# Layer 0 two groups ahead of the pairs, doubled tiles, and xe one group early in the second stage: a four-layer graph network on one core

## The chip, the cores and the metric

One core of one Trainium2 chip. The metric is the device time of one execution in microseconds (us). Times are medians of repeated executions.

## The reference, cut to what matters

Input: x, 128 graphs of 128 nodes with 128 features, and adj, an integer matrix of relations for each graph. Each of the four layers is x = x + layer(max(layernorm(x), 0), adj). Only the first two matter here:

```python
# layer 0: for each relation r = 1..7
mask = (adj == r); degree = max(mask.sum(axis=2), 1e-6)
agg += ((mask / degree) @ h) @ rel_weights[r]
out = relu(layernorm(agg + h @ self_w.T + self_b) * gamma + beta)

# layer 1: for all pairs (i, j) of nodes
D = abs(h[:, :, None, :] - h[:, None, :, :])
s = W2 . leaky(batchnorm(D @ W1.T + b1)) + b2      # batchnorm over ALL graphs and pairs
A = softmax(where(adj > 0, s, -9e15)); y = A @ h ...
```

The batch norm needs the statistics of all pairs before the first score. The kernel therefore makes the pairs twice: in the **first stage** for statistics (woven with layer 0), in the **second stage** for scores. Layers 2 and 3 are the **third stage**.

## The kernel before

Work goes in 32 groups of four graphs (k = 0 to 3). A scheduler orders the instructions of each engine when the kernel is built, and gives out buffers; it follows the order of the program only roughly. The parts that the change touches:

```python
def pre_norm(pool, src, mv=None, rs=None):
    ...
    h = pool.tile([P, G, P], F32, tag="hn", bufs=1, name="hn")
    norm(h, src, mv, rs)
    nc.vector.tensor_scalar(h, h, 0.0, None, op0=OP.max)
    return h

def around(pool, hT):                        # h with its first 64 nodes appended again
    xe = pool.tile([P, G, P + 2 * KH], F32, name="xe")
    nc.gpsimd.tensor_copy(xe[:, :, 0:P], hT)
    nc.gpsimd.tensor_copy(xe[:, :, P:], hT[:, :, 0:2 * KH])
    return xe

def pairwise(pool, xe, k, t):                # one pair step: 16 of them in a group
    d = pool.tile([P, 2, KC, P], F32, tag="d", bufs=3, name="d")
    ...
    eng = nc.gpsimd if t in ON_POOL else nc.vector      # ON_POOL = {1}: one d in four
    eng.tensor_tensor(d, ahead, x[...].to_broadcast(...), OP.subtract)
    nc.scalar.activation(d, d, AF.Abs)
    ...                                      # matmuls of d with w1T into hp (two buffers)

# layer0(g), cut: p0 has two buffers, unless a tile says bufs=1
for k in range(G):
    mask = p0.tile([P, 7, P], F32, name="mask", bufs=1)
    nc.vector.tensor_tensor(mask, adjT[...], rel[...], OP.is_equal)
    for r0, r1 in ((0, 3), (3, 7)):
        yield
        ...                                  # ph = h x relw (TensorE), hw = copy of ph (ScalarE)
        yield
        for r in range(r0, r1):
            nc.tensor.matmul(pa[:, r - r0, :], mask[:, r, :], hw[:, r - r0, :], ...)
        if r0 == 0:
            for r in range(7):               # the degrees
                nc.tensor.matmul(pa[:, 3, r:r + 1], mask[:, r, :], ones[:, 0:1], ...)
            ...                              # rdeg = 1 / max(degree, 1e-6) (VectorE)
        yield
        ...                                  # o += pa * rdeg (VectorE)

def pairs(g):
    xe = around(p0, HT[g])
    for k in range(G):
        yield from pair_stats(p0, xe, k, g * G + k)

for _ in layer0(0):
    pass
for g in range(NG):                          # 4 steps of layer 0 after each pair step
    _weave(pairs(g), layer0(g + 1) if g + 1 < NG else iter(()), 4)
```

## Time and profile before

| | before |
|---|---|
| median, us | 6777.6 |
| first stage: one group, steady (us between two xe copies) | 98.9 |
| VectorE busy in it / idle, us | 76.1 / 23.0 |
| second stage: one group, us | 64.94 |
| granted TensorE clock, steady first stage / second stage | 0.78 / 0.98 |

The views behind the table are in the prediction. In a timeline line, the columns are start and length in us, engine, line of the program, operation, tile written and tiles read, shapes, count, and in brackets the idle time of the engine before it and what ended it. Names of tiles come without the number of the buffer or the group. d holds the differences of pairs, hp their products with w1T and st the statistics of hp; pa holds the products with mask; hn is a normed tile, and lnrs and RS are the factors for a norm, which GpSimd makes.

### The profile page before, as it was taken

To read this page: it belongs to the slowest core of one execution; us is meant where nothing else is said; L and a number is where in the kernel's file an instruction comes from. 1 tells how busy PE (TensorE), PEld (TensorE's weight loads), DVE (VectorE), ACT (ScalarE), POOL (GpSimd) and SP (SyncE) were. 2 spreads that over 40 slices of the span, in tenths; PEclk is the share of its full clock that TensorE was granted. 3 is DMA by queue.
4 is the path that set the end of the run, shared out by engine and by line. 5 is a ranking of instruction groups with operands and counts; after the bars stand their busy time and mean duration, and the time that the engine had idled before them with its cause. 6 is when DMAs were issued, how large, how long until landed. Compare 5 with 4: busy or idle time off the path is not lost.

```text
span 6785.6 us, 58156 instructions
## 1 busy us (share of the span) xinstructions
PE 5091.2 (75%) x21510; PEld 2364.6 (35%) x21510; DVE 4731.7 (70%) x8187; ACT 3135.1 (46%) x2690; POOL 1536.1 (23%) x754
## 2 busy tenths in 40 slices
PE   5766776676677667666899999999999666666666
PEld 3323332332333233232222222222222355555555
DVE  5777777777777777778666666666666566666666
ACT  2333333333333333333677777777777422222222
POOL 2222222222222222222222222222222100000000
PEclk7887877787787778777899999999999877766667
DMA  0000000000000000000000000000000000000000
GB/s 21 5 10 10 8 7 10 10 5 10 10 8 7 10 10 5 10 7 5 15 16 16 16 16 19 16 16 17 17 18 16 16 13 13 13 13 13 13 13 8
DMA packets 108922, 81.32 MB, mean 12 GB/s; under 512 B 23392, under 2 KB 92256, under 8 KB 108640
## 3 DMA queue, kind: packets, MB, share of 16 engines
q1 hardware_dynamic: 91744, 69.20, 3.5%
q10 hardware_dynamic: 16896, 8.39, 0.4%
q8 instruction: 173, 2.83, 0.2%
q14 instruction: 109, 0.89, 0.0%
HBM read 47.36 MB, written 30.21 MB: 11 GB/s over the span
## 4 chain that ended last, share of the span: by engine, by line
PE 45%; DVE 30%; POOL 11%; ACT 9%; issue 4%; DMA 0%; SPq 0%; POOLq 0%; DVEq 0%; ACTq 0%
PE hp L193 20%; DVE d L187 9%; POOL d L187 6%; ACT d L189 5%; PE ps L376 5%; PE pa L264 3%; PE pv L526 3%; PE pa L261 3%; PE pt L165 3%; PE ph L255 2%; ACT z L372 2%; DVE st L203 2%; POOL xe L175 2%; DVE st L205 2%; PE pk L383 2%
## 5 line engine op out<-in xcount | busy, mean ns | idle before, releaser
L193 PE MATMUL hp<-d,w1T 128*64 128x512 f32 x8192 | 2553.4, 684 | 673.0 <-ACT d L189 541.7
L189 ACT ACTIVATE d<-d 128x2048 f32<-128x2048 f32 x1024 | 1938.8, 1906 | 935.6 <-POOL d L187 451.2
L187 DVE TENSOR_TENSOR d<-xe 128x2048 f32<-128x2048 f32 x768 | 1964.2, 2561 | 479.7 <-PE hp L193 477.1
L187 POOL TENSOR_TENSOR d<-xe 128x2048 f32<-128x2048 f32 x256 | 1096.6, 4284 | 3036.2 <-PE hp L193 3007.7
L193 PEld LDWEIGHTS hp<-d,w1T 128*64 128x64 f32 x8192 | 649.6, 152 | 2280.9 <-issue 1447.5
L372 ACT ACTIVATE z<-hp,bias,scale 128x1024 f32<-128x1024 f32 x512 | 608.4, 1200 | 352.9 <-PE hp L193 352.7
L376 PE MATMUL ps<-z,w2z 128*32 128x512 f32 x2048 | 508.4, 608 | 93.3 <-ACT z L372 93.3
L257 ACT COPY hw<-ph 128x384 f32<-128x384 f32 (+1 forms) x256 | 135.6, 530 | 857.0 <-PE ph L255 857.0
L203 DVE BATCH_NORM_STATS2 st<-hp 128x6 f32<-128x512 f32 x512 | 352.7, 689 | 229.6 <-PE hp L193 229.6
L261 PE MATMUL pa<-hw,mask 128*128 128x128 f32 x1792 | 325.7, 328 | 244.4 <-DVE mask L249 216.5
L261 PEld LDWEIGHTS pa<-hw,mask 128*128 128x128 f32 x1792 | 262.7, 221 | 514.4 <-issue 376.8
L135 POOL TENSOR_SCALAR lnrs<-lnmv 128x4 f32<-128x4 f32 x128 | 37.6, 294 | 1600.2 <-DVE lnmv L143 1600.2
L165 PE MATMUL pt<-ident,e 128*128 128x128 f32 x768 | 150.5, 344 | 292.4 <-ACT e L510 232.8
L165 PE MATMUL pt<-ident,hn 128*128 128x128 f32 x512 | 125.7, 392 | 298.7 <-DVE hn L159 234.5
L205 DVE BATCH_NORM_STATS2 st<-hp 128x6 f32<-128x512 f32 (+1 forms) x512 | 332.3, 649 | 0.0
L255 PE MATMUL ph<-relw,h 128*128 128x384 f32 (+1 forms) x512 | 305.1, 683 | 0.0
L270 DVE SCALAR_TENSOR_TENSOR o<-pa,rdeg,o 128x128 f32<-128x128 f32 x896 | 292.9, 336 | 12.5 <-PE pa L261 11.8
L148 DVE TENSOR_SCALAR hn<-x,lnmv,lnrs 128x128 f32<-128x128 f32 x384 | 111.8, 355 | 238.1 <-POOL lnrs L136 238.1
L264 PEld LDWEIGHTS pa<-ones,mask 128*128 128x128 f32 x1792 | 259.0, 229 | 0.0
L264 PE MATMUL pa<-ones,mask 128*128 128x1 f32 x1792 | 252.8, 270 | 0.0
L166 ACT COPY h<-pt 128x512 f32<-128x512 f32 x64 | 37.5, 586 | 432.2 <-PE pt L165 432.2
L175 POOL COPY xe<-h 128x512 f32<-128x512 f32 x64 | 154.3, 2410 | 353.9 <-DVE d L187 209.4
(154 smaller groups left out, 5222.6 us busy)
## 6 DMA issues: line engine op xcount, KB each, us to landing
x<-x SPq DMA_DIRECT2D x128, 256.0 KB, 2.4
u<-rows SPq DMA_DIRECT2D x32, 384.0 KB, 3.3
x<-in_x_dram SPq DMA_DIRECT2D x32, 256.0 KB, 2.7
adj<-in_adj_dram SPq DMA_DIRECT2D x32, 256.0 KB, 2.8
out_dram<-x ACTq DMA_DIRECT2D x32, 256.0 KB, 2.3
rows<-sk SPq DMA_DIRECT2D x32, 130.0 KB, 2.8
rows<-zero SPq DMA_DIRECT2D x2, 384.0 KB, 3.9
relw<-in_rel_w_dram SPq DMA_DIRECT2D x1, 448.0 KB, 4.0
```

Source lines behind the costliest of these rows:

```text
L165: nc.tensor.transpose(pt[:, k, :], src[:, k, :], ident)
L187: eng.tensor_tensor(d, ahead, x[:, None, None, :].to_broadcast([P, 2, KC, P]), OP.subtract)
L189: nc.scalar.activation(d, d, AF.Abs)
L193: nc.tensor.matmul(hp[64 * hh:64 * hh + 64, c:c + 512], w1T, d[:, hh, c:c + 512], start=True, stop=True)
L203: nc.vector.bn_stats(st[:, 2 * t, :], hp[:, 0:512])
L205: nc.vector.bn_stats(st[:, 2 * t + 1, :], hp[:, 512:1024 - P * last])
L255: nc.tensor.matmul(ph[:, 0:r1 - r0, :], hT[:, k, :], relw[:, r0:r1, :], start=True, stop=True)
L261: nc.tensor.matmul(pa[:, r - r0, :], mask[:, r, :], hw[:, r - r0, :], start=True, stop=True)
L264: nc.tensor.matmul(pa[:, 3, r:r + 1], mask[:, r, :], ones[:, 0:1], start=True, stop=True)
L270: nc.vector.scalar_tensor_tensor(o[:, k, :], pa[:, r - r0, :], rdeg[:, r:r + 1], o[:, k, :], op0=OP.mult, op1=OP.add)
L372: nc.scalar.activation(z, hp, AF.Prelu, bias=bias1, scale=scale1[:, 0:1], alpha=0.01)
L376: nc.tensor.matmul(ps[q:q + 32, :], w2z[:, w:w + 32], z[:, 512 * c:512 * c + 512], start=j < 4, stop=j >= 4, skip_group_check=True)
```

## The change

The intent: run layer 0 two groups ahead of the pairs, so that xe is ready long before it is needed; give the tiles of layer 0 a second buffer; and make xe of the second stage a group early.

```diff
+AHEAD = 2
...
-        h = pool.tile([P, G, P], F32, tag="hn", bufs=1, name="hn")
+        h = pool.tile([P, G, P], F32, tag="hn", name="hn")
...
-        xe = pool.tile([P, G, P + 2 * KH], F32, name="xe")
+        xe = pool.tile([P, G, P + 2 * KH], F32, name="xe", bufs=AHEAD + 1)
...
-                mask = p0.tile([P, 7, P], F32, name="mask", bufs=1)
+                mask = p0.tile([P, 7, P], F32, name="mask")
# ... the same for adj, adjf, adjT and o
...
             transpose(hT, h)
+            yield
+            XE[g] = around(p0, hT)

         def pairs(g):
-            xe = around(p0, HT[g])
+            xe = XE.pop(g)
...
-        for _ in layer0(0):
-            pass
+        XE = {}
+        for g in range(AHEAD):
+            for _ in layer0(g):
+                pass
         for g in range(NG):
-            _weave(pairs(g), layer0(g + 1) if g + 1 < NG else iter(()), 4)
+            _weave(pairs(g), layer0(g + AHEAD) if g + AHEAD < NG else iter(()), 4)
...
+        XE = {0: around(p1, HT[0])}            # second stage
         def group_scores(g):
-            xe = around(p1, HT[g])
+            if g + 1 < NG:
+                XE[g + 1] = around(p1, HT[g + 1])
+            xe = XE.pop(g)
```

Since `pre_norm` is shared, hn is doubled in the later stages too.

More of the change, by code (lines that the diff above doesn't have):

```diff
@@ L227, in layer0 @@
             nc.sync.dma_start(x, a["x"][bs].rearrange("b t c -> t b c"))
-            adj = p0.tile([P, G, P], I32, name="adj", bufs=1)
+            adj = p0.tile([P, G, P], I32, name="adj")
             nc.sync.dma_start(adj, a["adj"][bs].rearrange("b t s -> t b s"))
@@ L232, in layer0 @@
             yield
-            adjf = p0.tile([P, G, P], F32, name="adjf", bufs=1)
+            adjf = p0.tile([P, G, P], F32, name="adjf")
             nc.vector.tensor_copy(adjf, adj)
@@ L237, in layer0 @@
             yield
-            adjT = p0.tile([P, G, P], F32, name="adjT", bufs=1)
+            adjT = p0.tile([P, G, P], F32, name="adjT")
             transpose(adjT, adjf)
             yield
-            o = p0.tile([P, G, P], F32, name="o", bufs=1)
+            o = p0.tile([P, G, P], F32, name="o")
             po = sm("po")
```

## The prediction

> **What bounds the kernel now.** I began with busy time in long stretches, to see the stages. Columns: matmul, weight load, VectorE, ScalarE, GpSimd busy us (with counts), granted TensorE clock, DMA share, GB/s.
>
> ```profile
> core 0: us, PE busy (x) PEld busy (x) DVE busy (x) ACT busy (x) POOL busy (x), PEclk, DMA share, GB/s
> 140.00:3100.00 2960.00, 2071.99 (x8259) 924.07 (x8255) 2275.45 (x4159) 1069.73 (x808) 804.49 (x389) 0.79 0.03 8
> 3250.00:5430.00 2180.00, 1968.42 (x8186) 646.84 (x8183) 1401.62 (x1443) 1601.76 (x1176) 581.32 (x197) 0.98 0.06 16
> 5560.00:6785.00 1225.00, 793.47 (x4031) 647.27 (x4029) 786.02 (x2038) 340.17 (x582) 73.55 (x108) 0.69 0.04 12
> ```
>
> The first stage (layer 0 woven with the pair statistics, to about 3219 us) has no full engine: VectorE 77%, matmuls 70%. The second is matmul bound (90%, clock 0.98). The third is a chain of short steps. The change is meant for the first, so I next read the chain of work that ended last around one group boundary.
>
> ```profile
> 1739.71 1.13 PE pt L165 x4
> ...
> 1740.86 0.59 ACT h L166
> ...
> 1741.51 4.21 POOL xe L175
> 1745.72 0.34 POOL xe L176
> 1746.07 4.15 POOL d L187
> ...
> 1750.24 3.72 ACT d L189 x2
> ...
> 1754.00 6.52 PE hp L193 x16
> ```
>
> This is a start-up that each group pays: the last transpose of layer 0 for group g+1 lands on ScalarE, GpSimd copies it to xe, GpSimd makes a difference d, ScalarE takes its absolute value, and then sixteen matmuls run at 0.41 us each. The same matmuls take 0.24 us each once running (eight in 1.94 us). xe copies follow each other at 98.9 us (1741.51, then 1840.56), 31 times. One such period, and VectorE's waits in it (us in total, times, longest):
>
> ```profile
> 1741.50:1840.56 99.06, 69.39 (x276) 30.96 (x276) 76.10 (x140) 35.74 (x27) 26.94 (x14) 0.78 0.03 9
> ```
> ```profile
> DVE st L203 <- PE hp L193: 7.0, 7, 1.7
> DVE hn L148 <- POOL lnrs L136: 5.2, 1, 5.2
> DVE rdeg L266 <- PE pa L264: 5.1, 4, 2.4
> DVE mask L249 <- PE pa L261: 3.4, 2, 2.2
> DVE o L148 <- POOL lnrs L136: 1.2, 1, 1.2
> DVE hn L148 <- POOL RS L136: 0.9, 1, 0.9
> ```
>
> VectorE is busy 76.1 of 99.1 us and idle 23. About 9.7 us of that idle lies at the boundary (the 5.2, 1.2, 0.9, and 2.3 of the waits for hp); the other 13 lie in the middle, in layer 0's exchange with TensorE. Busy time itself holds waiting. In the timeline of both engines:
>
> ```profile
> 1765.15 5.07 DVE L187 TENSOR_TENSOR d<-xe 128x2048 f32<-128x2048 f32 x1
> ```
> ```profile
> 1763.54 4.54 POOL L187 TENSOR_TENSOR d<-xe 128x2048 f32<-128x2048 f32 x1 [12.02 <-PE hp L193]
> ```
>
> A VectorE d normally takes 2.2 us. This one took 5.07, because GpSimd's d ran to 1768.1 and VectorE needed 2.2 us after that. The d at 1817.98 (4.64 us) is the same; with a norm slowed beside GpSimd's mask (1.60 instead of 1.11 us), such stalls are 5.7 us a period. Net VectorE work is thus 76.1 - 5.7 = 70.4 us.
>
> **What the Trainium skill says.** "SBUF — State Buffer", section "Who interferes with whom": a VectorE instruction with two SBUF inputs and a GpSimd instruction that reads SBUF exclude each other for a whole instruction. The trace agrees (5.07 against 2.2 us; and the xe copy above took 4.21 us behind two VectorE d, 0.61 us in the second stage). "TensorE: Matmul & The Clock Gate", section "What's actually happening": idle TensorE falls to half clock and needs a few us of work to come back. The trace agrees: 0.41 us a matmul after 5.28 us of idle, 0.24 in dense stretches. "Perfetto Trace Analysis", section "Optimization Strategy": a consistent bubble can mean too few buffers. Here it is at first order not a lack of buffers but of distance, since layer 0 of g+1 ends just when pairs of g end.
>
> **The change part by part.** No instruction is added or removed in the first stage. It makes layer 0 run two groups ahead, copies xe at the end of layer 0 (three xe buffers), and doubles hn, adj, adjf, adjT, o and mask. The diff does not show the order, because a scheduler fixes it, so I compared the built instruction order of both kernels. In the changed one, a steady period on GpSimd reads: d of k=0, 1, 2, then two rsqrt and the mask of layer 0, the xe copy for two groups on, a third rsqrt, then d of k=3. VectorE's first d of a group no longer follows the xe copy of that group, two masks are made back to back before TensorE needs them, and the norm of the next layer 0 stands among the last pair steps.
>
> (1) Boundary. 9.7 us of VectorE idle a group should go nearly whole: xe is at hand a group early, and the 5.2 us wait for lnrs arose because GpSimd did xe and d first.
> (2) Middle. The waits for mask (3.4) should go with the second mask buffer; those for rdeg and hp (5.1 and 4.7) should shrink, since they are waits for TensorE at half clock or held up by masks. I leave 5 us of the 13.
> (3) Port. GpSimd still does four d of 4.17 us and now meets a denser VectorE. In the pairs-only end of the stage (3138 to 3205 us) each k has one VectorE d of 4.1 to 5.1 us, a stall of up to 2.9. By walking the new order by hand with the durations above, I find stalls at three of the four d (2.7, 1.5, 1.6), plus some at mask and norm, together 7 to 8 us instead of 5.7.
> Sum: 70.4 + 7.6 + 5 = 83 us a period. The hand walk, with all matmuls at full speed, came to 80; 83 allows for half-clock stretches.
>
> The whole stage. Before: pairs of group 0 start at about 82 us, those of group 31 end at about 3219, so 3137 us. After, from the same start: group 0 has to carry two layers 0 (groups 1 and 2), at 21 us of VectorE work and some TensorE latency more, so 83 + 28; groups 1 to 29 take 83; groups 30 and 31 have pairs alone, at 16.5 us per k, so 66 each; 5 for seams. 111 + 29 x 83 + 132 + 5 = 2655. Gain 3137 - 2655 = 482 us.
>
> (4) Second stage. The xe copy there waits 7.2 us for a buffer, but takes 0.6 us, ends 4 us before the next GpSimd d, and is not on the chain. Bringing it a group early is worth nothing. With hn doubled, VectorE's 2.0 us wait for py per group disappears, and the norm (1.4 us) moves to a place where VectorE idled 2.25 us for hp; both are beside a TensorE that is 90% busy. In the built order, TensorE and ScalarE are unchanged from the start of that stage on. I count 0, plus or minus 15 us.
> (5) Third stage. It gets the second hn too; its order is the same on all engines, and no wait for the hn buffer shows there. 0.
>
> 6777 - 482 = 6295.
>
> **The rivals.**
> A, only the boundary goes. The layer 0 exchange in the middle keeps its 13 us of idle. For it: most of the order there is unchanged, and rdeg waits for TensorE, not for a buffer. Against: mask waits are 3.4 of the 13, and matmuls run at half clock after gaps, which shrink together. Period 70.4 + 6 + 13 = 89, stage 30 x 89 + 165 = 2835, time 6475.
> B, GpSimd's queue becomes the wait. d of k=3 stands behind two rsqrt, the mask and the xe copy, which itself waits for the last transpose and then for three VectorE d in a row (6.6 us). If the pairs starve there, the bubble is only moved from the boundary into k=2. For it: the queue is in order and 98.9 us periods show how firmly such a chain locks. Against: three VectorE d are already made ahead of it, enough for about 10 us of pairs. Period 87 to 90, time about 6415 to 6505.
> C, VectorE fills up entirely. Period 76 (net work plus stalls), 30 x 76 + 165 = 2445, time 6085. An in-order queue that waits for TensorE rarely gets there; pairs alone keep 1.9 us of idle per k even without layer 0.
> D, nothing: the transfers and copies were hidden anyway. The chain passes through xe at each of 31 boundaries, so I hold this for the second stage only.
>
> **Range and chances.** Each us of the period is 30 us of the time. Periods from 79 to 88 give 6175 to 6445; I state 6180 to 6450. A gain of 2% is 136 us, which a period under 94.5 gives; even rival B is well below. Faster 0.95, same 0.04, slower 0.01.
>
> **What would show it.** Step 1: distance between xe copies near 83 us instead of 98.9; the chain no longer has xe; no 5 us wait for lnrs. Step 2: mask gone from the list of waits, clock of the stage above 0.79. Step 3: VectorE busy 77 to 79 us a period, with d of 4 to 5 us. Steps 4 and 5: the second stage stays at about 64.9 us a group, the third at its length. I am wrong if VectorE waits at k=2 or 3 for hp while GpSimd's xe copy stands over 5 us, if the granted clock stays below 0.8, or if the second stage moves by more than 30 us.

## The result

6699.9 us (6693.6 to 6712.5) against 6777.6 us. Ratios here are the mean time of one kernel's fast runs over that of the other's of the same rounds, so not quite the ratio of the medians; here it is 0.9888 (95% interval 0.9871 to 0.9906). That is 1.1% faster: outside the predicted range, and by the 2% measure the same.

From the traces, by stage (us):

| | before | after | difference |
|---|---|---|---|
| last pair statistic of the first stage starts at | 3215.6 | 3127.2 | -88.4 |
| from there to the first z of the second stage | 24.9 | 26.4 | +1.5 |
| first z to last z | 2087.1 | 2099.4 | +12.3 |
| last z to first yT of the third stage | 28.3 | 28.1 | -0.2 |
| from there to the end | 1429.7 | 1429.6 | -0.1 |

A steady group of the first stage takes 95.57 us instead of 98.9. First its busy times (columns as in the prediction), then VectorE's waits in it:

```profile
1155.70:1251.27 95.57, 63.40 (x276) 28.10 (x276) 78.58 (x140) 35.58 (x27) 30.75 (x14) 0.86 0.03 9
```
```profile
DVE st L204 <- PE hp L194: 7.1, 6, 2.4
DVE rdeg L267 <- PE pa L265: 5.0, 3, 2.4
DVE hn L149 <- POOL lnrs L137: 1.5, 1, 1.5
DVE o L149 <- POOL lnrs L137: 1.2, 1, 1.2
DVE mask L250 <- PE pa L262: 1.1, 1, 1.1
```

VectorE is idle for 17.0 us (95.57 - 78.58), where 5 were predicted. Against before, the 5.2 us wait for lnrs became 1.5 and the mask waits went from 3.4 to 1.1; the waits for hp and rdeg did not move. VectorE's busy time rose from 76.1 to 78.6 us with the same 140 instructions, so some of them now take longer. The timelines of GpSimd and VectorE show what became of the lnrs wait:

```profile
1155.70 6.87 POOL L176 COPY xe<-h 128x512 f32<-128x512 f32 x1 [3.48 <-ACT h L167]
...
1163.57 1.04 POOL L137 TENSOR_TENSOR lnrs<-lnrs,mhalf 128x4 f32<-128x4 f32 x1
1164.58 4.16 POOL L188 TENSOR_TENSOR d<-xe 128x2048 f32<-128x2048 f32 x1
```
```profile
1155.42 6.68 DVE L188 TENSOR_TENSOR d<-xe 128x2048 f32<-128x2048 f32 x3
...
1164.64 4.69 DVE L149 TENSOR_SCALAR hn<-x,lnmv,lnrs 128x128 f32<-128x128 f32 x3 [1.48 <-POOL lnrs L137]
...
1181.76 3.19 DVE L160 TENSOR_SCALAR hn<-hn 128x512 f32<-128x512 f32 x1
...
1232.37 3.41 DVE L188 TENSOR_TENSOR d<-xe 128x2048 f32<-128x2048 f32 x1
```

The xe copy, 0.6 us of work, stands behind three VectorE d. Then GpSimd's d starts 0.06 us before VectorE's norm, and the norm, about 0.9 us of work, takes 4.69. That looks like rival B of the prediction, and it was my first theory.

### The profile page after: what moved, and what is told of

Its sections match the earlier page's. It is cut to its first block, busy times and chain, and to the rows that moved or that the text cites. A ratio compares the mean times of both kernels' runs of the same rounds, so it can differ in the third digit from the quotient of the medians.

```text
span 6710.7 us, 58135 instructions
## 1 busy us (share of the span) xinstructions
PE 4948.1 (74%) x21510; PEld 2296.2 (34%) x21510; DVE 4916.2 (73%) x8187; ACT 3131.5 (47%) x2690; POOL 1642.9 (24%) x754
## 4 chain that ended last, share of the span: by engine, by line
PE 44%; DVE 36%; POOL 9%; ACT 8%; issue 3%; DMA 0%; SPq 0%; POOLq 0%; DVEq 0%; ACTq 0%
PE hp L194 18%; DVE d L188 12%; POOL d L188 6%; ACT d L190 4%; PE ps L382 4%; PE pa L262 3%; DVE hn L160 3%; PE pv L536 3%; PE pa L265 3%; PE pt L166 3%; PE ph L256 3%; DVE hn L149 2%; DVE st L206 2%; POOL lnrs L137 2%; PE pk L389 2%
## 5 line engine op out<-in xcount | busy, mean ns | idle before, releaser
L194 PE MATMUL hp<-d,w1T 128*64 128x512 f32 x8192 | 2505.1, 673 | 666.9 <-ACT d L190 605.2
L188 DVE TENSOR_TENSOR d<-xe 128x2048 f32<-128x2048 f32 x768 | 1841.9, 2405 | 358.8 <-PE hp L194 358.2
L188 POOL TENSOR_TENSOR d<-xe 128x2048 f32<-128x2048 f32 x256 | 1126.4, 4400 | 2925.4 <-PE hp L194 2886.8
L262 PE MATMUL pa<-hw,mask 128*128 128x128 f32 x1792 | 278.7, 298 | 82.7 <-ACT hw L258 48.0
L262 PEld LDWEIGHTS pa<-hw,mask 128*128 128x128 f32 x1792 | 230.0, 199 | 289.9 <-ACT hw L258 203.6
L149 DVE TENSOR_SCALAR hn<-x,lnmv,lnrs 128x128 f32<-128x128 f32 x384 | 225.5, 644 | 123.6 <-POOL lnrs L137 123.5
L176 POOL COPY xe<-h 128x512 f32<-128x512 f32 x64 | 222.6, 3478 | 329.8 <-DVE d L188 201.7
L271 DVE SCALAR_TENSOR_TENSOR o<-pa,rdeg,o 128x128 f32<-128x128 f32 x896 | 290.1, 339 | 14.4 <-PE pa L262 13.8
L166 PEld LDWEIGHTS pt<-ident,hn 128*128 128x128 f32 x512 | 81.6, 196 | 626.8 <-DVE hn L160 334.8
L256 PE MATMUL ph<-relw,h 128*128 128x384 f32 (+1 forms) x512 | 266.0, 603 | 0.0
L160 DVE TENSOR_SCALAR hn<-hn 128x512 f32<-128x512 f32 x160 | 244.7, 1529 | 1.6
```

The costliest lines, as they stand in the source:

```text
L149: nc.vector.tensor_scalar(dst[:, k, :], src[:, k, :], mv[:, k, 0:1], rs[:, k:k + 1], op0=OP.subtract, op1=OP.mult)
L166: nc.tensor.transpose(pt[:, k, :], src[:, k, :], ident)
L188: eng.tensor_tensor(d, ahead, x[:, None, None, :].to_broadcast([P, 2, KC, P]), OP.subtract)
L194: nc.tensor.matmul(hp[64 * hh:64 * hh + 64, c:c + 512], w1T, d[:, hh, c:c + 512], start=True, stop=True)
L256: nc.tensor.matmul(ph[:, 0:r1 - r0, :], hT[:, k, :], relw[:, r0:r1, :], start=True, stop=True)
```

## The experiments

**The theories.** PORT: the distance freed the boundary, but GpSimd's queue (xe copy, then the d of k=3) and the lock between the two engines take the gain back. MIDDLE: the period is set by layer 0's exchange between TensorE, ScalarE and VectorE; the distance gave nothing, and what was gained came from the doubled tiles. The first four kernels ran together; so did the next four, and the last four. Each was timed in three rounds against the kernel before.

### Doubled tiles alone

```diff
# kernel before; second and third stage untouched
-mask = p0.tile([P, 7, P], F32, name="mask", bufs=1)
+mask = p0.tile([P, 7, P], F32, name="mask")
# the same for adj, adjf, adjT, o, and for hn in the first stage
```

> The kernel before with hn, adj, adjf, adjT, o and mask doubled in the first stage; layer 0 still one group ahead, second and third stage untouched. Theory MIDDLE (the gain of the whole change came from the second mask buffer, which takes mask waits of 3.4 us a group out of layer 0's exchange with TensorE; the distance gave nothing): 6690 to 6720 us, period 96 us or less. Theory PORT (the distance freed the boundary, but the xe copy and GpSimd's fourth d then lock VectorE out and take most of it back): the tiles alone give at most the mask waits of some groups, 6740 to 6775 us, and the 5.2 us wait for lnrs stays.

6670.2 us, ratio 0.9842 (0.9827 to 0.9856): 104 us faster than before, more than the whole change. The period is 95.57 us, the same as with the whole change. PORT expected at most 34; MIDDLE had the period right, but its range (6690 to 6720 us) is missed by 20 us on the fast side.

### Two groups ahead alone

```diff
# changed kernel
-mask = p0.tile([P, 7, P], F32, name="mask")
+mask = p0.tile([P, 7, P], F32, name="mask", bufs=1)
# the same for adj, adjf, adjT, o and hn; the second stage's xe as before
```

> The changed kernel with layer 0 two groups ahead and three xe buffers, but every other tile of the first stage single as before, second and third stage as before. PORT: most of the gain is here, 6690 to 6730 us, the xe copy again takes over 4 us behind VectorE's d, period 95 to 97 us. MIDDLE: at most 30 us faster than before, 6745 to 6777 us, since mask is single again.

6791.1 us, ratio 1.0019 (1.0002 to 1.0035): not faster at all, and 14 us above MIDDLE's range too. Its period alternates between 98.9 and 99.0 us, as before, and VectorE's waits in a period are those of the kernel before:

```profile
DVE st L204 <- PE hp L194: 6.9, 7, 1.6
DVE hn L149 <- POOL lnrs L137: 5.2, 1, 5.2
DVE rdeg L267 <- PE pa L265: 5.1, 4, 2.4
DVE mask L250 <- PE pa L262: 3.4, 2, 2.2
```

So the 5.2 us wait for lnrs was never a matter of distance. The built order of GpSimd's queue in the kernel before says why. Cut to the d and the xe copies of one period, with the groups written in:

```
d  k=0, 1, 2   from xe of group 16
xe copy        of group 17
d  k=3         from xe of group 16
d  k=0, 1, 2   from xe of group 17
```

The scheduler had already put the copy for the next group ahead of the last d of this one. In the chain that the prediction shows, the xe copy at 1741.51 and the d at 1746.07 follow each other in GpSimd's queue, but the d reads the older xe. It was no group's start-up. The trace of the kernel before agrees:

```profile
1740.78 4.47 DVE L187 TENSOR_TENSOR d<-xe 128x2048 f32<-128x2048 f32 x2
```

The second of these two VectorE d, done at 1745.25, is the first d of the same k as GpSimd's d at 1746.07; ScalarE takes the two one after the other from 1750.24. It was finished before the xe copy was (1746.07), so this k cannot read the new xe. What the copy costs by standing in that queue of the kernel before was not tested.

### The later stages alone

```diff
# kernel before; first stage untouched
+XE = {0: around(p1, HT[0], 3)}              # three buffers
 def group_scores(g):
-    xe = around(p1, HT[g])
+    if g + 1 < NG:
+        XE[g + 1] = around(p1, HT[g + 1], 3)
+    xe = XE.pop(g)
# and hn with two buffers in the second and third stage
```

> The kernel before with the second stage's xe one group early and hn doubled in the second and third stage; first stage untouched. Between the traces the second stage grew from 64.94 to 65.27 us a group, the third did not change. If that growth belongs to these lines: 6785 to 6795 us, period of the second stage 65.3 us. If it came from the end of the first stage (another phase at entry): 6777 us as before.

6793.9 us, ratio 1.0025 (1.001 to 1.004), period of the second stage mostly 65.27 us: this part costs 20 us. Tiles (-104), distance (+17) and later stages (+20) sum to -67; the whole change has -78. They add within 11 us.

### The xe copy on ScalarE

```diff
# changed kernel, first stage only
-XE[g] = around(p0, hT)
+XE[g] = around(p0, hT, nc.scalar.copy)      # both copies of around
```

> The changed kernel with the first stage's xe copy made by ScalarE, which is idle over 60% there, instead of GpSimd. PORT: the 6.9 us copy behind three VectorE d becomes about 1 us, GpSimd's fourth d starts about 7 us earlier, period 95.6 to 86-90 us, 6430 to 6560 us. MIDDLE: the copy was only a stand-in, the wait turns up elsewhere: period 94 to 96 us, 6660 to 6710 us.

6700.0 us, ratio 0.9886; period 95.56 us, as the changed kernel. ScalarE makes the copy in 0.62 us:

```profile
1142.64 0.62 ACT L177 COPY xe<-h 128x512 f32<-128x512 f32 x1
```
```profile
1150.23 0.23 POOL L136 TENSOR_SCALAR lnrs<-lnmv 128x4 f32<-128x4 f32 x1 [11.03 <-DVE lnmv L144]
...
1151.55 4.16 POOL L189 TENSOR_TENSOR d<-xe 128x2048 f32<-128x2048 f32 x1
```

GpSimd is now free for 11 us before lnrs, and its d starts as late as ever, because lnrs stands ahead of it in the queue and waits for VectorE. The long copy filled idle time. PORT in this form falls, for the changed kernel.

### One tile doubled: mask

```diff
# kernel before
-mask = p0.tile([P, 7, P], F32, name="mask", bufs=1)
+mask = p0.tile([P, 7, P], F32, name="mask")
```

> The kernel before with one edit: two buffers for mask. The tiles alone gave 104 us (6774 to 6670), with a period of 95.57 instead of 98.9 us. Theory MASK: the second mask buffer is what counts (mask waits 3.4 to 1.1 us a group): 6665 to 6700 us. Rival HN: the second hn buffer counts (the wait of the norm for lnrs fell from 5.2 to 1.5 us a group): then mask alone gives little, 6740 to 6775 us.

6668.1 us, ratio 0.9838 (0.9824 to 0.9853). One edit gives all that the six doubled tiles give, with the same period (95.57 us) and the same list of waits as the whole change, the lnrs wait of 1.5 us included. The second hn buffer is worth nothing: with two masks the scheduler orders GpSimd's queue differently, and lnrs now stands before the d instead of behind it:

```profile
1009.17 6.88 POOL L175 COPY xe<-h 128x512 f32<-128x512 f32 x1 [3.48 <-ACT h L166]
...
1016.73 0.23 POOL L135 TENSOR_SCALAR lnrs<-lnmv 128x4 f32<-128x4 f32 x1 [0.34 <-DVE lnmv L143]
...
1018.05 4.16 POOL L187 TENSOR_TENSOR d<-xe 128x2048 f32<-128x2048 f32 x1
```

So the second mask does two things: of the 6.0 us of idle time that VectorE lost a period, 3.7 are the wait for lnrs and 2.3 the waits for mask. The period fell by only 3.4, since busy time rose by 2.5. No run tells what each of the two is worth alone.

### Layer 0 spread more evenly, one and two groups ahead

In both earlier kernels layer 0 has some 37 steps, four after each pair step, so it is emitted beside the first 9 or 10 of 16 pair steps.

```diff
# e6: doubled tiles, one ahead. e7: the changed kernel, two ahead. In both:
-    for _ in main:
-        for _ in range(steps):
-            next(side, None)
+    done = 0
+    for n, _ in enumerate(main):
+        while done < steps * (n + 1):
+            next(side, None)
+            done += 1
...
-_weave(pairs(g), layer0(...) ..., 4)
+_weave(pairs(g), layer0(...) ..., 2.5)
```

> The kernel with doubled tiles only (layer 0 one group ahead), but 2.5 instead of 4 steps of layer 0 between two pair steps, so layer 0 is spread over about 15 of the 16 pair steps instead of 9. Theory MIDDLE: the 17 us of VectorE idle a group that are left come from bunching layer 0 (five to seven pair steps share VectorE and TensorE with all of it, the others have none): period 95.6 to 84-90 us, 6350 to 6510 us. But with one group ahead the xe copy now comes at the very end of the group, so the boundary may cost up to 10 us a group again: then 6550 to 6700 us. Rival FLOOR (idle is inherent in the chain of waits of one layer 0, however it is spread): 6650 to 6700 us.

6519.5 us, ratio 0.962 (0.9605 to 0.9634): 3.8% faster than before, the best kernel. Periods alternate; two of them, and VectorE's waits in both:

```profile
1064.50:1245.40 180.90, 125.51 (x552) 55.81 (x552) 152.03 (x279) 71.46 (x54) 58.19 (x27) 0.84 0.03 9
```
```profile
DVE st L205 <- PE hp L195: 15.8, 13, 4.4
DVE hn L150 <- POOL lnrs L138: 5.3, 2, 4.1
DVE rdeg L268 <- PE pa L266: 4.0, 4, 1.2
```

A period is now 90.4 us; the rdeg wait fell from 5.0 to 2.0 us a period and the mask wait is gone. Of the 5.1 us that the period fell, idle time gave half (17.0 to 14.4 us) and busy time the other half (78.6 to 76.0), which holds the stalls behind GpSimd; so the spread lessened collisions too, and this run does not tell the two apart. The period is at the edge of what MIDDLE expected (84 to 90), the time 10 us above its range.

> The changed kernel (two ahead, doubled tiles) with 2.5 steps instead of 4. MIDDLE: period 84 to 90 us, 6370 to 6540 us, and here the distance should be worth something: faster than the same with one ahead if the xe copy at the end of the group costs anything there. FLOOR: 6680 to 6720 us.

6543.2 us, ratio 0.9657 (0.9642 to 0.9671): close to MIDDLE's range, 3 us above it. It is 24 us slower than with one group ahead, of which the later stages account for 20. Even with layer 0 ending late in the group, the distance gains nothing.

### No d on GpSimd

```diff
# doubled tiles only; first stage (in effect)
-eng = nc.gpsimd if t in ON_POOL else nc.vector
+eng = nc.vector
```

> The kernel with doubled tiles only, all sixteen d of a group on VectorE in the first stage (GpSimd makes none there). It takes away every collision of the two engines' d (about 8 us of stalled VectorE a group) and d of 4.2 us, and adds four d of 2.2 us, 8.8 us of VectorE work. Theory PORT (collisions set the period): 6400 to 6600 us, period 87 to 93. MIDDLE: VectorE's stalls are exchanged for work of the same size: 6640 to 6720 us, period 94 to 97.

6617.2 us, ratio 0.9769 (0.9752 to 0.9785); 93.9 us a period over two. The busy times of these two periods:

```profile
1077.71:1265.46 187.75, 131.03 (x552) 57.30 (x552) 157.98 (x287) 71.83 (x54) 23.82 (x19) 0.84 0.03 9
```

All collisions of d with GpSimd are gone, and the gain is 1.7 us a period. But VectorE now makes four more d of 2.2 us: it is busy for 79.0 us a period, as before (78.6), with 8.8 us of work in place of 8.2 us of stalls. MIDDLE's range is missed by 23 us, PORT's by 17. The run shows that GpSimd's help with d is worth nothing at 4 steps; what the stalls alone cost, it does not show.

### Layer 0's exchange made shorter

```diff
# changed kernel; result wrong on purpose (relative error 0.35)
-for r in range(7):
-    nc.tensor.matmul(pa[:, 3, r:r + 1], mask[:, r, :], ones[:, 0:1], start=True, stop=True)
-nc.vector.tensor_scalar(rdeg, pa[:, 3, 0:7], 1e-6, None, op0=OP.max)
+nc.vector.tensor_scalar(rdeg, ones[:, 0:7], 1e-6, None, op0=OP.max)
```

> Wrong result on purpose: the changed kernel without the 28 products of mask with ones in a group (layer 0's degrees; 5.8 us of TensorE a group), the reciprocal taken of a constant instead. Nothing else is changed. Theory MIDDLE (layer 0's exchange of TensorE, ScalarE and VectorE lies on the path that sets the period; the chain of the changed kernel has these products with 5.7% of a period): period 95.6 to 88-91 us, about 6500 to 6580 us. Rival PORT (the path is the one through GpSimd's queue and the locked norm, TensorE catches up in its idle time): at most 2 us a period, 6640 to 6700 us.

6527.0 us, 173 us faster than the changed kernel; periods of 89.5 to 92.2 us, over five 90.8 on average, so 4.8 less. The products removed took about 1.46 us for each k, 5.8 us a group. In the changed kernel's chain they stand like this, twice in this stretch:

```profile
1206.28 0.86 PE pa L262 x6
1207.14 1.46 PE pa L265 x14
...
1213.25 0.49 ACT hw L258
...
1213.78 0.94 PE pa L262 x6
1214.72 1.47 PE pa L265 x14
...
1216.21 0.17 DVE rdeg L267
```

Four fifths of the time taken out of TensorE came off the period, although TensorE has 32 us of idle in each. This shows that layer 0's exchange is on the path, as MIDDLE says. It is not a test of TensorE's time alone: with the products went the wait, since rdeg no longer reads what TensorE makes, and that wait was 5.0 us a period. VectorE's waits without the products, in 90 us: rdeg is off the list, as it must be, and the waits for hp are about as they were.

```profile
DVE st L204 <- PE hp L194: 7.7, 6, 2.4
DVE hn L149 <- POOL lnrs L137: 1.5, 1, 1.5
DVE o L149 <- POOL lnrs L137: 1.2, 1, 1.2
...
```

### hn doubled in the later stages alone

```diff
# kernel before, second and third stage only (in effect)
-h = pool.tile([P, G, P], F32, tag="hn", bufs=1, name="hn")
+h = pool.tile([P, G, P], F32, tag="hn", bufs=2, name="hn")
```

> The kernel before with only hn doubled in the second and third stage (the second stage's xe as before). The two together cost 14.9 us in the second stage. If the moved norm does it: period 65.27 us, 6785 to 6797 us. If the third xe buffer and the early copy do it: 64.94 us, 6773 to 6780 us.

6800.4 us, ratio 1.0034 (1.0017 to 1.005), 65.27 us a group; the time is 3 us above the range expected for the moved norm, 20 above the other. The moved norm is the cost; the early xe copy costs nothing. The two traces show how, first before (VectorE, then GpSimd), then the changed kernel:

```profile
4091.88 2.72 DVE L187 TENSOR_TENSOR d<-xe 128x2048 f32<-128x2048 f32 x1 [4.66 <-PE hp L193]
```
```profile
4088.26 4.19 POOL L187 TENSOR_TENSOR d<-xe 128x2048 f32<-128x2048 f32 x1 [4.32 <-PE hp L193]
```
```profile
4068.28 4.45 DVE L160 TENSOR_SCALAR hn<-hn 128x512 f32<-128x512 f32 x1
4072.66 2.28 DVE L188 TENSOR_TENSOR d<-xe 128x2048 f32<-128x2048 f32 x1
```
```profile
4068.26 4.19 POOL L188 TENSOR_TENSOR d<-xe 128x2048 f32<-128x2048 f32 x1 [4.32 <-PE hp L194]
```

The last part of the norm (about 0.4 us of work) starts just after GpSimd's d and is held until that ends. VectorE's next d then follows behind it and ends 6.68 us after GpSimd's d began; before, it ended 6.34 us after (4091.88 + 2.72 - 4088.26). That is the 0.33 us a group, some 10 us in all; the rest of the 20 us was not located.

### The helpers together, and the weave alone

```diff
# e11: kernel before + mask doubled + 2.5 steps + all first-stage d on VectorE
# e12: kernel before + 2.5 steps
```

> The three things that helped, together, on the kernel before: two mask buffers (-106 us), 2.5 instead of 4 steps (-150 us on top of the tiles), all first-stage d on VectorE (-53 us on top of the tiles); layer 0 one group ahead, later stages untouched. If they add: 6460 to 6480 us. If spreading layer 0 already took what the d on VectorE gave, or VectorE becomes full (its work would be about 79 us a group): 6510 to 6560 us.

6557.7 us, ratio 0.9675: inside the range for gains that do not add, and slower than the best by 38 us. With layer 0 spread out, moving d to VectorE is a loss (the best has five more tiles doubled, which gave nothing with 4 steps).

> The kernel before with 2.5 instead of 4 steps and single tiles. If bunching is the cause of the idle time, and mask waits are one symptom of it: 6510 to 6560 us, close to the same with doubled tiles (6520). If the second mask buffer is a gain of its own: 6600 to 6640 us.

6672.2 us, ratio 0.9843 (0.9828 to 0.9858). Both guesses missed: the first by over 100 us, the second by 32. Spreading alone gives 106 us, the second mask alone gives 110, and with the tiles doubled spreading gives another 151. Together (with all six tiles doubled) they give 258, some 43 us more than the sum: they help each other. With the weave alone VectorE still waits 10.6 us a period for hp, 5.3 for rdeg and 1.9 for mask; why one buffer costs so much there was not followed further.

## Why the prediction was wrong, point by point

- **Reading of the bound, wrong.** "This is a start-up that each group pays" is the step that failed first. It took two neighbours in the chain for a data dependence. They were neighbours in a queue: the copy was for the next group, the d for this one. So step 1's 9.7 us were not at a boundary that distance could remove. Distance alone left the period at 98.9 and all waits as they were; its cost is 17 us by itself, just clear of noise. In the whole change the first z of the second stage comes 25.6 us later than with the tiles alone (3153.6 against 3128.0). Some 14 of these lie before the first xe copy (68.0 against 81.9 us), and they are not shown to be a cost of distance: the kernel before and the two runs that change only the later stages have the same first stage, and their first copies are at 81.6, 78.6 and 71.7 us. The prediction's other reason for the 5.2 us, that GpSimd made the d before lnrs, was right; what put lnrs first was the second mask.
- **Step 2 (middle), mis-sized, and the largest miss.** Of 13 us idle it kept 5; VectorE's whole idle time is 17.0 us instead of those 5. Mask waits went to 1.1, not 0; those for rdeg (5.1 to 5.0) and hp (7.0 to 7.1) stayed. The hand walk that gave 80 us had seven degree products at 0.75 us, about half of what the trace shows (fourteen rows, 1.46 us at full speed). The run without them shows that such time, with the wait for it, counts for four fifths. Rival A named this outcome ("only the boundary goes", 89 us); in fact part of the middle went, and the boundary was none.
- **Step 3 (port), right in size by luck.** Predicted 7 to 8 us of stalls, 5.8 of them on three d; measured 78.6 - 70.4 = 8.2. But 3.8, 2.8 and 0.5 us fall on norms (4.69, 3.19 and 1.60 us long) and only 1.1 on a d (3.41 us long). What the stalls cost is open: without GpSimd's d, work of the same size took their place.
- **Sum.** 70.4 + 8.2 + 17.0 = 95.6 instead of 83. The rest of the stage's account held: with 95.6 in it, it gives 3033 us from 82 us on; from the traces it is 3137 - 88 = 3049.
- **Step 4 (second stage), at the edge.** "0, plus or minus 15": it grew by 12.3 us. Over all traces of this case, first z to last z takes 2099 to 2106 us in the six with hn doubled there and 2080 to 2090 in the eight without, 16 us more on average. The xe copy was indeed worth nothing. The norm did not move into idle time; it moved beside a GpSimd d.
- **Step 5 (third stage), right.** 1429.7 to 1429.6 us.
- **Rival B** (GpSimd's queue becomes the wait) looked right in the trace of the changed kernel and was wrong: freeing the queue of the copy changed nothing. Its warning sign came true all the same: at k=3 VectorE waits for hp (1.4 and 2.4 us) while the xe copy stands for 6.87.
- **The signs named.** xe copies at 83 us: no, 95.6. xe off the chain: yes, in the period read. lnrs wait gone: from 5.2 to 1.5, for a reason that has nothing to do with distance. Clock above 0.79: yes, 0.86. VectorE busy 77 to 79 us: yes, 78.6. A sign that comes true is no proof of the step it was named for.

## What to carry to other kernels

Where a scheduler orders the queues, look in the built order whether a prefetch already happens before paying for more distance, and check that two neighbours in a chain of waits use the same buffer. For a repeating idle pattern, look first for the single-buffered tile that two engines hand to each other, and double that one alone; here six doubled tiles gave no more than one. Then read the built order again, since a buffer changes it. Side work woven into a main loop should be spread over the whole of it: an uneven weave left 151 us here that doubling six tiles did not recover.

## What the Trainium skill lacked or had wrong

- "Perfetto Trace Analysis", section "Optimization Strategy": its remark that a consistent bubble can mean too few buffers was right here, and the prediction talked it away; one mask buffer was worth 110 us. Its advice to interleave regimes gives no word on the evenness of the weave, worth 151 us here.
- "SBUF — State Buffer", section "Who interferes with whom": it has VectorE's tensor_scalar among the instructions that can take the shared ports, and the trace agrees: the norm is one, and took 4.69 us for 0.9 us of work beside GpSimd's d. It does not say that back-to-back instructions of one engine keep the other out between them: the 0.61 us xe copy waited for all three VectorE d in a row, 6.87 us.
- "TensorE: Matmul & The Clock Gate": agrees (0.41 against 0.24 us a matmul). It does not say that an fp32 product stands in the trace as two rows: seven one-column products took 1.46 us in fourteen rows, 104 ns each.
- No page says how much of a stall on a shared port counts in the time of a kernel, and no run here shows it: 8.2 us of stalls a period, exchanged for 8.8 us of VectorE work, gave 1.7 us.
